# Layer 3's conditioning block: the second half of its routing one step sooner, and three row scatters per step

## The chip, the cores and the metric

The kernel runs on one core of one Trainium2 chip. The metric is device time in microseconds (us) for one execution of the whole program; shown is the median of several executions. The engines of a core each work through a queue of their own in order: TensorE (PE in the profile; its weight loads stand apart as PEld), VectorE (DVE), ScalarE (ACT), GpSimd (POOL) and SyncE (SP), which here only issues DMAs and reads registers. They meet through semaphores.

## The reference

Four layers follow one another on 2048 tokens of 256 channels. Each is `x = x + ffn(cond(x))`, and nearly all of these are mixtures of experts. The one that matters here is the condition of layer 3, cut to its core:

```python
shared = silu(xf @ w1) * (xf @ w3) @ w2              # all tokens, hidden width 512
s = sigmoid(concat([xf, tf], -1) @ router_W)         # 8 experts
_, topk_idx = top_k(s + router_bias, 2)
s_sel = take_along_axis(s, topk_idx, axis=1)
gates = s_sel / (s_sel.sum(axis=1, keepdims=True) + 1e-9)
h = gelu(einsum('nc,ech->enh', xf, W1e), approximate=False)
y = einsum('enh,ehc->enc', h, W2e)                   # hidden width 256
routed = einsum('ne,enc->nc', combine, y)            # combine: gates at the chosen two
out = (shared + routed) / 3
```

Every token goes through one shared expert and two routed ones of eight. The layers before it are complete when it starts, and the last expert layer, which sends each token to one of 16 experts, needs its result.

## The kernel before, in words

Tokens lie in SBUF twice: by channel (`XT`, for matmuls over channels) and by token (`Xt`, for rows). The 2048 tokens are 16 tiles of 128, and four blocks of 512.

A routed expert gets its tokens sorted. The kernel works out for each token and each of its two experts a row number in a DRAM buffer `xbuf`, scatters the token rows there (32 scatters: 16 tiles times two experts, each one indirect DMA that POOL issues), and then walks over 39 slots of 128 rows. A slot loads its rows (`xs`, line 297, issued by SP), turns them by a PE transpose (`ps_cm`, line 364), multiplies with its expert's weights (`cph`, line 1678, and `cpo`, line 1685) and scatters the result to another buffer, `tbuf`. The first `xs` load waits for all 32 scatters to have landed, since any of them may have written its rows.

To hide routing and scatters, they are spread over the shared expert. It takes blocks of 512 tokens; layer 3 runs three of the four blocks ahead of the slots (`lead` is 3) and the last one behind them. Its hidden width of 512 is four pieces of 128, so that a block is four steps, and three blocks are twelve. A step (`_shared`, lines 1413 to 1456) is: four matmuls for the gate (`spg`) and the up projection (`spu`), line 1440; a SiLU on ACT (`ssg`, line 1445); and the multiply on DVE (`sa`, line 1449). The down projection (`spo`, line 1426) of a step comes one step later, behind the next step's `spg` and `spu`, so that the multiply has time. Behind each `spo`, `_shared` calls a hook: the n-th hook comes in PE's queue behind the n-th `spo`, and so behind the `spg` and `spu` of step n + 1. The last step of a block is the exception (hooks 4, 8 and 12): its `spo` and hook follow at once, ahead of the next block.

The hooks drive a `Lead` (lines 303 to 333). The routing is a generator in two parts, split by `yield`. Part 1 computes the logits on PE (`ps_lt`), the sigmoid on ACT (`l3c_lt`), a transpose back (`l3c_pl`), and then on DVE the scores, the top two by MAX8 and FIND_INDEX8 (lines 173 and 175), one-hot masks `l3c_oh`, their sum `l3c_M` (line 1804) and its running sums over 16 tiles `l3c_cum` (line 193). Part 2 begins with matmuls on `l3c_M` and `l3c_cum` that count the rows before each token (`l3c_R` and `l3c_cnt`, lines 204 to 209), and goes on with some forty small DVE operations: the row numbers (`l3c_rows`), the expert of each slot (`l3c_eid`) and the gates. `Lead` gets the hooks at which the parts are issued, `at`, and a number of scatters per step, `per`:

```python
def hook(self, f, mul, mm):
    self.n += 1
    if self.n in self.at:
        self.part()
        if not self.at:
            for _ in range(min(self.per, len(self.sends))):
                self.sends.pop(0)()
    elif self.n > self.late:
        for _ in range(min(self.per, len(self.sends))):
            self.sends.pop(0)(mul)
```

At the hook of the last part the first `per` scatters are sent as soon as the row numbers are there; at each hook behind it `per` more, each of which also waits for that step's multiply `mul`. `late` is the largest number in `at`. With `(1, 3), 4`, part 1 is issued at hook 1, part 2 and four scatters at hook 3, and four at each of hooks 4 to 10.

What is left on the queues around this: SP reads the expert numbers of all slots into registers and loads the first slots' weights (`_slot_weights`, lines 1568 to 1577), then loads biases of the last layer over columns of `XT` that the shared blocks have finished with (line 2171, four loads of 128 KB for each block), and fetches `xs`. A planner turns the program into the engines' queues: it goes by the program's order where operands are ready by its own estimate of times, and lets later instructions pass where they are not. A queue's order is then fixed, and each engine keeps to it.

The other two layers that use `Lead` have eight pieces to a block and `(2, 4), 2`.

Of the kernel before, what the change touches and what calls it, by code (L numbers as in the profile page):

```python
# [78 lines left out]
def _bc(ap, axis, shape):  # L79
    return ap.unsqueeze(axis).to_broadcast(shape)  # L80
# [86 lines left out]
def _top(nc, pool, lg, E, name):  # L167

    m8 = pool.tile([P, NT, 8], F32, name=name + "_m8", tag="m8")
    ix = pool.tile([P, NT, 8], U32, name=name + "_ix", tag="ix")  # L170
    ixf = pool.tile([P, NT, 8], F32, name=name + "_ixf", tag="ixf")
    for t in range(NT):
        nc.vector.max(m8[:, t, :], lg[:, t, :])
    for t in range(NT):
        nc.vector.max_index(ix[:, t, :], m8[:, t, :], lg[:, t, :])
    nc.vector.tensor_copy(ixf, ix)
    return m8, ixf


def _one_hot(k, pool, ixf, n, E, name, tag=None):  # L180
    oh = pool.tile([P, NT, E], F32, name=name, tag=tag or name)
    k.nc.vector.tensor_tensor(oh, _bc(k.iota[:, 0:E], 1, [P, NT, E]),
                              ixf[:, :, n:n + 1].to_broadcast([P, NT, E]), ALU.is_equal)
    return oh


def _running(k, pool, M, E, name):

    nc = k.nc
    cum = pool.tile([P, NT + 1, E], F32, name=name + "_cum", tag="r_cum")  # L190
    nc.vector.memset(cum[:, 0, :], 0.0)
    for t in range(NT):
        nc.vector.tensor_add(cum[:, t + 1, :], cum[:, t, :], M[:, t, :])
    return cum
# [51 lines left out]
def _rows_of(k, pool, oh, pos, E, name, tag=None):  # L246

    nc = k.nc
    t = pool.tile([P, NT, E], F32, name=name + "_w", tag="rt")
    nc.vector.tensor_mul(t, oh, pos)  # L250
    f = pool.tile([P, NT], F32, name=name + "_f", tag="r_f")
    nc.vector.tensor_reduce(f, t, AX.X, ALU.add)
    u = pool.tile([P, NT], U32, name=name, tag=tag or name)
    nc.vector.tensor_copy(u, f)
    return u
# [1118 lines left out]
def _logits(k, psum, pool, src, w, E, name, dst, func=None, bias=None):  # L1374


    nc = k.nc
    ps = psum.tile([P, TB], F32, name="ps_lt", tag="mm")
    for c in range(2):
        for g in range(NB):  # L1380
            nc.tensor.matmul(ps[32 * g:32 * g + 32, :], w[:, c, :], src[:, c, g * TB:(g + 1) * TB],
                             start=c == 0, stop=c == 1, skip_group_check=True)
    lt = pool.tile([P, TB], F32, name=name + "_lt", tag="lt")
    if func is None:
        nc.scalar.copy(lt[:, 0:256], ps[:, 0:256])
        nc.vector.tensor_copy(lt[:, 256:TB], ps[:, 256:TB])
    else:
        nc.scalar.activation(lt, ps, func, bias=bias)
    pl = psum.tile([P, 4, 4, 32], F32, name=name + "_pl", tag="mm")
    for j in range(4):  # L1390
        nc.tensor.transpose(pl[:, j].rearrange("p g r -> p (g r)"), lt[:, j * P:(j + 1) * P], k.ident)
    nc.vector.tensor_copy(dst.rearrange("p (g j) e -> p j g e", g=4), pl[:, :, :, 0:E])
# [113 lines left out]
def _name_rows(k, rows, ixf, base):  # L1506

    k.nc.vector.tensor_scalar_add(rows[:, :, D], k.tok2, float(base))
    k.nc.vector.tensor_copy(rows[:, :, D + 1], ixf[:, :, 0])
# [162 lines left out]
def _gelu_products(k, pool, psum):  # L1672

    nc = k.nc

    def products(xT, R1, R2):
        ph = psum.tile([P, 2, P], F32, name="cph", tag="mm")
        made = [nc.tensor.matmul(ph[:, f, :], R1[:, c, f * P:(f + 1) * P], xT[:, c, :], start=c == 0,  # L1678
                                 stop=c == 1) for f in range(2) for c in range(2)]
        h = pool.tile([P, 2, P], F32, name="ch", tag="sg")  # L1680
        nc.scalar.activation(h, ph, AF.Gelu)
        yield made
        yield None
        po = psum.tile([P, D], F32, name="cpo", tag="o", bufs=2)
        made = [nc.tensor.matmul(po, h[:, f, :], R2[:, f, :], start=f == 0, stop=f == 1) for f in range(2)]  # L1685
        y = pool.tile([P, D], F32, name="ys", bufs=4)
        nc.vector.tensor_copy(y, po)
        yield made
        yield y
    return products  # L1690
# [93 lines left out]
def _cond_moe(k, name, wr, bias, W1, W3, W2, nf, hold, R1, R2, gate_mult, final, lead, next=None):  # L1784

    nc, A, XT, HT, Xt, Ht = k.nc, k.A, k.XT, k.HT, k.Xt, k.Ht
    rp, pool, psum = k.rp, k.pool, k.psum
    E, T, NS = 8, P, 39
    base = 0 if next else 8192
    w, rb = k.small[wr], k.small[bias]  # L1790
    sets = []
    for i in range(4):
        r = k.ring.take(1, hold).rearrange("p (n c f) -> p n c f", n=2, f=D)
        sets.append([(r[:, 0], A[R1]), (r[:, 1], A[R2])])
    def routing(lead_):
        s = rp.tile([P, NT, E], F32, name=name + "_s", tag="s")
        _logits(k, psum, rp, XT, w, E, name, s, AF.Sigmoid, k.small[wr, "b"])
        sel = rp.tile([P, NT, E], F32, name=name + "_sel", tag="lg")
        nc.vector.tensor_tensor(sel, s, _bc(rb, 1, [P, NT, E]), ALU.add)
        _, ixf = _top(nc, rp, sel, E, name)  # L1800
        _name_rows(k, k.Xr, ixf, base)
        oh = [_one_hot(k, rp, ixf, n, E, name + "_oh%d" % n, "oh%d" % n) for n in range(2)]
        M = rp.tile([P, NT, E], F32, name=name + "_M", tag="M")
        nc.vector.tensor_add(M, oh[0], oh[1])
        cum = _running(k, rp, M, E, name)
        yield
        pos, eid, of, _ = _route(k, rp, psum, M, cum, E, T, NS, len(sets), name)
        rows = [_rows_of(k, rp, oh[n], pos, E, name + "_rows%d" % n, "rows%d" % n) for n in range(2)]
        k.x.begin()
        lead_.sends = k.x.paced(k.Xr, rows)  # L1810

        nc.vector.tensor_mul(M, M, s)
        den = rp.tile([P, NT], F32, name=name + "_den", tag="den")
        nc.vector.tensor_reduce(den, M, AX.X, ALU.add)
        big = rp.tile([P, NT], F32, name=name + "_big", tag="big")
        nc.vector.tensor_single_scalar(big, den, 1e-9, ALU.is_gt)
        nc.vector.tensor_scalar_add(den, den, 1e-9)
        nc.vector.reciprocal(den, den)
        nc.vector.tensor_mul(den, den, big)
        nc.vector.tensor_scalar(big, big, -0.5, 0.5, ALU.mult, ALU.add)  # L1820
        gate = []
        for n in range(2):
            nc.vector.tensor_mul(oh[n], oh[n], s)
            g = rp.tile([P, NT], F32, name=name + "_g%d" % n, tag="g%d" % n)
            nc.vector.tensor_reduce(g, oh[n], AX.X, ALU.add)
            nc.vector.tensor_mul(g, g, den)
            nc.vector.tensor_add(g, g, big)
            nc.vector.tensor_scalar_mul(g, g, gate_mult * final)
            gate.append(g)
        lead_.made = gate, eid, of  # L1830

    def shared(tb, hook=None, mid=None, added=lambda: False):
        po = _shared(k, pool, psum, XT, tb, W1, W3, W2, nf, hook, mid)
        for i in range(2):
            t = tb * 4 + i * 2
            if added():
                nc.vector.scalar_tensor_tensor(Ht[:, t:t + 2, :], po[i], final, Ht[:, t:t + 2, :],
                                               ALU.mult, ALU.add)
            else:
                nc.scalar.activation(Ht[:, t:t + 2, :], po[i], AF.Copy, scale=final)  # L1840

    lead_ = Lead(k, routing, *((2, 4), 2) if nf == 8 else ((1, 3), 4))
    def hook(f, mul, mm):
        if k.late:
            k.late.pop(0)(k.silu, mul)
        lead_.hook(f, mul, mm)

    for tb in range(lead):
        shared(tb, hook)
    gate, eid, of = lead_.finish()  # L1850
    k.t.begin()
    slots = Series(k, Slots(k, pool, psum, of, base), 0, NS)
    for i in range(NS):
        slots.slot(i, _gelu_products(k, pool, psum), lambda: _slot_weights(k, eid, i, sets, E))
    slots.close()
    if next:
        next.begin()
    c = Tokens(k, pool, psum, gate, Ht, HT, nf, next)
    for tb in range(lead, NB):
        c.there = tb * 4  # L1860
        shared(tb, c.hook, c.hook, lambda: c.added >= tb * 4 + 4)
    c.there = NT
    k.ring.drop(hold)
    if next:
        next.finish(c)
    else:
        c.finish()
# [583 lines left out]
```

## Time and profile before

| | us |
|---|---|
| time, median of 3 runs | 1504.56 (1503.55 to 1510.06) |
| the profiled execution | 1522.55 |
| its span in the profile | 1520.8 |
| PE busy | 1448.3 (95%) |
| DVE busy | 468.9 (31%) |
| POOL busy | 280.9 (18%) |

The shares are of the span. Ends of matmuls are modelled, so a busy PE is not one at its peak. The mean clock that was granted to TensorE in the profiled execution was 0.977 of full speed. A line of the order in time reads: start in us from the span's start, duration in us, engine, source line, operation, tile written and tiles read, shapes and count; in brackets the time that the engine stood idle before it, and what ended that. "issue" there means that nothing the profile shows was waited for. "SPq" is a DMA issue on SP, so its duration is that of issuing and not of the transfer.

Layer 3's condition starts its shared blocks at 1176.0 us and its slots at 1258.4 us in that execution.

### The profile page before, as it was taken

Reading aid. Unit: us, or ns where it says so; the run is one execution under the profiler, and the core shown is the slowest. Engines: PE = TensorE matmul, PEld = TensorE weight load, DVE = VectorE, ACT = ScalarE, POOL = GpSimd, SP = SyncE. Lnnn points to the kernel's source line nnn. Section 1 sums busy time; section 2 is a strip of 40 time slices with the busy share of each in tenths; the row PEclk is TensorE's granted clock in tenths of the full one; section 3 lists DMA queues with packets and bytes.
Section 4 is the critical chain, followed back from the end, with each engine's and each line's share of the span. In section 5 each row is a group of like instructions: output and inputs, shape, how many; then the busy total and the mean of one; then the engine's idle time right before and its main releaser. Section 6 shows DMA issues by size and latency. Waiting matters only on the chain. (4 is left out here: it accounts for less than half of the span.)

```text
span 1520.8 us, 23724 instructions
## 1 busy us (share of the span) xinstructions
PE 1448.3 (95%) x8660; PEld 1023.3 (67%) x8660; DVE 468.9 (31%) x1606; ACT 304.9 (20%) x642; POOL 280.9 (18%) x317
## 2 busy tenths in 40 slices
PE   8999998999999999999999999999999969998897
PEld 4543333645557886555899999999976538864675
DVE  4432222325212444411211111111114404456432
ACT  3221111213111122211111111111112212135222
POOL 0400001200431440142010101010100253410442
PEclk9999999999999999999999999999999989998899
DMA  9669993943311772151235145246327438671470
GB/s 315 214 195 308 348 331 115 298 101 126 115 52 53 244 230 82 53 191 49 73 134 188 39 177 189 80 154 223 125 95 234 147 89 260 217 234 65 156 253 16
DMA packets 179856, 249.69 MB, mean 164 GB/s; under 512 B 17207, under 2 KB 132159, under 8 KB 179728
## 3 DMA queue, kind: packets, MB, share of 16 engines
q1 hardware_dynamic: 160064, 208.16, 42.5%
q0 software_dynamic: 14176, 36.63, 6.7%
q10 hardware_dynamic: 5488, 3.25, 0.7%
q8 instruction: 73, 1.20, 0.3%
q14 instruction: 55, 0.45, 0.1%
HBM read 284.86 MB, written 48.00 MB: 219 GB/s over the span
## 5 line engine op out<-in xcount | busy, mean ns | idle before, releaser
L281 POOL DMA_INDIRECT tbuf<-ys,sdst x114 | 112.2, 984 | 507.9 <-ACT ys L1714 382.6
L1426 PE MATMUL spo<-ring,sa 128*128 128x256 f32 x768 | 182.3, 382 | 12.9 <-DVE sa L1449 12.9
L1426 PEld LDWEIGHTS spo<-ring,sa 128*128 128x128 f32 x768 | 145.6, 191 | 63.0 <-issue 32.7
L1449 DVE TENSOR_TENSOR sa<-ssg,spu 128x512 f32<-128x512 f32 x96 | 65.8, 686 | 297.7 <-PE spu L1440 246.5
L1707 DVE TENSOR_TENSOR fa<-fsg,fpu 128x512 f32<-128x512 f32 x72 | 49.5, 688 | 316.2 <-PE fpu L1702 316.2
L1702 PE MATMUL fpg<-xsT,ring 128*128 128x128 f32 x1152 | 140.4, 275 | 0.7 <-issue 0.7
L1702 PE MATMUL fpu<-xsT,ring 128*128 128x128 f32 x1152 | 140.4, 275 | 0.0
L1702 PEld LDWEIGHTS fpg<-xsT,ring 128*128 128x128 f32 x1152 | 137.0, 192 | 2.7 <-issue 0.9
L1702 PEld LDWEIGHTS fpu<-xsT,ring 128*128 128x128 f32 x1152 | 134.4, 192 | 0.0
L1711 PE MATMUL fpo<-ring,fa 128*128 128x256 f32 x576 | 130.3, 379 | 0.0
L1445 ACT ACTIVATE ssg<-spg 128x512 f32<-128x512 f32 x96 | 57.3, 597 | 316.1 <-PE spg L1440 260.3
L1711 PEld LDWEIGHTS fpo<-ring,fa 128*128 128x128 f32 x576 | 106.7, 190 | 13.0
L1440 PE MATMUL spg<-HT,ring 128*128 128x512 f32 x192 | 95.9, 614 | 6.6 <-issue 3.5
L1440 PE MATMUL spu<-HT,ring 128*128 128x512 f32 x192 | 92.6, 605 | 0.0
L1440 PE MATMUL spg<-XT,ring 128*128 128x512 f32 x192 | 90.9, 595 | 0.1
L1440 PE MATMUL spu<-XT,ring 128*128 128x512 f32 x192 | 90.2, 592 | 0.0
L1678 PE MATMUL cph<-xsT,ring 128*128 128x128 f32 x624 | 84.2, 278 | 4.4 <-DMA ring<-in_L_r 2.7
L1678 PEld LDWEIGHTS cph<-xsT,ring 128*128 128x128 f32 x624 | 75.8, 191 | 8.6 <-issue 2.9
L1685 PE MATMUL cpo<-ring,ch 128*128 128x256 f32 x312 | 79.9, 380 | 0.0
L1706 ACT ACTIVATE fsg<-fpg 128x512 f32<-128x512 f32 x72 | 43.0, 597 | 171.7 <-PE fpg L1702 171.7
L1440 PEld LDWEIGHTS spu<-HT,ring 128*128 128x128 f32 x192 | 37.4, 196 | 46.7 <-issue 46.0
L1440 PEld LDWEIGHTS spu<-XT,ring 128*128 128x128 f32 x192 | 36.5, 190 | 45.9 <-issue 45.0
(580 smaller groups left out, 1637.4 us busy)
## 6 DMA issues: line engine op xcount, KB each, us to landing
ring<-in_L_w SPq DMA_DIRECT2D x108, 1024.0 KB
ring<-in_L_r SPq DMA_DIRECT2D x96, 512.0 KB
ring<-in_L_r SPq DMA_DIRECT2D x156, 256.0 KB
xs<-xbuf SPq DMA_DIRECT2D x138, 129.0 KB
ring<-in_L_W SPq DMA_DIRECT2D x32, 512.0 KB
yt<-tbuf SPq DMA_DIRECT2D x48, 256.0 KB
xbuf<-ACC SPq DMA_DIRECT2D x1, 3096.0 KB
ring<-in_L_s SPq DMA_DIRECT2D x6, 512.0 KB
```

What stands on the lines that cost most here:

```text
L281: i = k.nc.gpsimd.indirect_dma_start(out=self.ap, out_offset=bass.IndirectOffsetOnAxis(ap=idx, axis=0), in_=rows, in_offset=None, **end)
L1426: mm = nc.tensor.matmul(po[g // 2][:, g % 2, :], a[:, g * P:(g + 1) * P], W2[:, f, :], start=f == 0 and g % 2 == 0, stop=f == nf - 1, skip ...
L1440: mm = nc.tensor.matmul(ps, W[:, c, f * P:(f + 1) * P], X[:, c, cols], start=c == 0, stop=c == 1)
L1445: k.silu = nc.scalar.activation(sg, pg, AF.Silu)
L1449: mul = nc.vector.tensor_mul(a, sg, pu)
L1678: made = [nc.tensor.matmul(ph[:, f, :], R1[:, c, f * P:(f + 1) * P], xT[:, c, :], start=c == 0, stop=c == 1) for f in range(2) for c in ra ...
L1685: made = [nc.tensor.matmul(po, h[:, f, :], R2[:, f, :], start=f == 0, stop=f == 1) for f in range(2)]
L1702: made = [nc.tensor.matmul(ps[:, j, :], W[:, c, (f0 + j) * P:(f0 + j + 1) * P], xT[:, c, :], start=c == 0, stop=c == 1) for ps, W in ((pg, ...
L1706: nc.scalar.activation(sg, pg, AF.Silu)
L1707: nc.vector.tensor_mul(a[:, f0:f0 + 4, :], sg, pu)
L1711: made = [nc.tensor.matmul(po, a[:, f, :], W2[:, f, :], start=f == 0, stop=f == 4 * nh - 1) for f in range(4 * nh)]
```

## The change

One line of `_cond_moe` changes the arguments of `Lead` for layer 3's condition (the case `nf == 4`); layer 2's condition keeps its own.

```diff
-    lead_ = Lead(k, routing, *((2, 4), 2) if nf == 8 else ((1, 3), 4))
+    lead_ = Lead(k, routing, *((2, 4), 2) if nf == 8 else ((1, 2), 3))
```

Part 2 of the routing is issued at hook 2 in place of hook 3. Three scatters are sent there, three at each of hooks 3 to 11, and the two that remain at hook 12; before, it was four at each of hooks 3 to 10. No instruction is added or removed.

## The prediction

> **What bounds the kernel now.** I read the page first, then the order of instructions by time on each engine around layer 3's condition (about 1176 to 1262 us), then the waits. The page says that TensorE (PE) is the busy engine:
>
> ```profile
> span 1520.8 us, 23724 instructions
> PE 1448.3 (95%) x8660; PEld 1023.3 (67%) x8660; DVE 468.9 (31%) x1606; ACT 304.9 (20%) x642; POOL 280.9 (18%) x317
> ```
>
> So a change that touches no arithmetic can only move the places where PE stands. PE in this stage (start us, duration, engine, line, operation, tiles, count, idle before it and what ended that):
>
> ```profile
> 1191.83 1.89 PE L1426 MATMUL spo<-ring,sa 128*128 128x256 f32 x8
> 1193.56 1.88 PE L1440 MATMUL spg<-XT,ring 128*128 128x512 f32 x4
> 1195.28 1.88 PE L1440 MATMUL spu<-XT,ring 128*128 128x512 f32 x4
> ...
> 1198.72 0.39 PE L204 MATMUL l3c_R<-l3c_M,before 128*128 128x128 f32 x2
> ...
> 1232.74 3.78 PE L1426 MATMUL spo<-ring,sa 128*128 128x256 f32 x8 [12.55 <-DVE sa L1449]
> ...
> 1258.38 0.85 PE L364 MATMUL ps_cm<-ident,xs 128*128 128x128 f32 x4 [0.96 <-DMA xs<-xbuf]
> ```
>
> The reader should see three things. A step (spg, spu, spo) takes 5.16 us. The routing's second part begins with l3c_R, which follows the third step's spo. And the slots begin at 1258.38 with a wait for xs, rows that have come through DRAM: what ends last before the slots is the scatters, their landing and the load, though shared matmuls run until 1257.4 here.
>
> VectorE (DVE) shows what l3c_R needs:
>
> ```profile
> 1193.40 0.68 DVE L1449 TENSOR_TENSOR sa<-ssg,spu 128x512 f32<-128x512 f32 x1
> 1193.99 0.28 DVE L1804 TENSOR_TENSOR l3c_M<-l3c_oh,l3c_oh 128x128 f32<-128x128 f32 x1
> 1194.31 3.18 DVE L193 TENSOR_TENSOR l3c_cum<-l3c_cum,l3c_M 128x8 f32<-128x8 f32 x16
> 1197.41 0.68 DVE L1449 TENSOR_TENSOR sa<-ssg,spu 128x512 f32<-128x512 f32 x1
> ...
> 1254.07 0.69 DVE L1449 TENSOR_TENSOR sa<-ssg,spu 128x512 f32<-128x512 f32 x1 [4.47 <-PE spu L1440]
> ```
>
> The running sums are done at 1197.49, only 1.23 us before l3c_R starts. The scatters on GpSimd (POOL):
>
> ```profile
> 1203.11 1.04 POOL L281 DMA_INDIRECT xbuf<-Xt,l3c_rows  x1 [76.24 <-DVE l3c_ef L238]
> 1204.45 0.96 POOL L281 DMA_INDIRECT xbuf<-Xt,l3c_rows  x1 [0.30 <-issue]
> ...
> 1227.19 0.96 POOL L281 DMA_INDIRECT xbuf<-Xt,l3c_rows  x1 [0.30 <-issue]
> 1232.96 0.95 POOL L281 DMA_INDIRECT xbuf<-Xt,l3c_rows  x1 [4.82 <-DVE sa L1449]
> ...
> 1250.13 0.96 POOL L281 DMA_INDIRECT xbuf<-Xt,l3c_rows  x1 [0.30 <-issue]
> ```
>
> They run back to back, 1.263 us apart ((1227.19-1204.45)/18), so four fill 5.05 of a step's 5.16 us. The queue of DMA issues on SP:
>
> ```profile
> 1248.27 2.21 SPq L2171 DMA_DIRECT2D XT<-in_L_b  x4
> 1256.25 1.75 SPq L297 DMA_DIRECT2D xs<-xbuf  x4
> ```
>
> The last scatter left POOL at 1251.09; xs could be fetched only at 1256.25, 5.16 us later, with four bias loads in between on the same DMA engines.
>
> **A stall to take out first.** PE's 12.55 us wait hangs on ACT, whose wait the list of waits calls "remote", 19.1 us. In the trace's record of semaphore updates PE posts nothing from 1214.49 to 1231.35, then three updates within 0.1 us, although its matmuls were issued by 1218.30; SP's register loads slow at the same time from 0.56 to 2 to 3 us a triple. I take this for something that recording brings. The profiled execution took 1522.55 us against a median of 1504.56, 18 us more, and no other stall of that kind is in the trace. Without it everything on PE after 1232 comes 12.71 (1232.74 against 1218.30 + 1.73) + 1.85 (spo x8 took 3.58 to the next start, not 1.73) + 0.29 (spg x4) = 14.85 us earlier. POOL would not have waited (its releases stay ahead of it), so the 32nd scatter ends at 1204.45 + 30 x 1.263 + 0.96 = 1243.3, while shared matmuls end at 1257.42 - 14.85 = 1242.6. SP's remaining triples (35 x 0.56 us after 1213) would be over by about 1233 and the four bias loads behind them drained long before. So the scatters bound this stage in the runs that are timed. Their landing is then like layer 2's, where no bias load is near: last one out at 454.45, fetch at 456.20, 1.75 us. Slots begin at 1243.3 + 1.75 + 2.13 (1258.38-1256.25) = 1247.2, about 11 us before the profile's. The other 7 us of the 18 I leave to recording, unplaced; the sum is made as a difference in this stage and put on the median.
>
> **The change part by part.**
>
> *Part 2 at hook 2.* No instruction is added: 3 groups of matmuls and about 5.9 us of small DVE operations (1199.14 to 1205.0) move. In program order l3c_R would come behind the spo at 1191.83, at 1193.56. Its operand comes at 1197.49. If PE's queue holds it there, PE stands 3.93 us, and behind it stand spg and spu of the fourth step and their spo. If the planner sees that the sums are late, it puts spg and part of spu first; it does such things, since in layer 2 it put two l2f_pl at 623.36, two spg at 623.63 and two more l2f_pl at 624.50. A hint of its clock: it put the third step's sa (1193.40) just ahead of l3c_M, so it held that operand, whose spu ends 3.4 us after part 1's last transposes, ready by then; on the chip that point is 4.9 us after them. Its DVE is thus fast by some 1 to 2 us, and l3c_R lands early by about that. I take s = 1.0 us of PE standing, ends 0 and 3.93, nearer the planned placement. The scatters' start then moves by little: l3c_R to first scatter is 4.39 us (1203.11-1198.72), so from 1197.5 they begin at about 1202.0, 1.1 us sooner and not a step. The eid loads and the eight weight loads of SP start sooner by as much; the weights are not needed until the slots, over 40 us later, so that is hidden; if it weren't it would be a gain.
>
> *Three per step.* Before, 4 at hook 3 and 4 at each of hooks 4 to 10. After, 3 at hook 2, 3 at each of 3 to 11 (30), the last two at hook 12, waiting for the last multiply of the block. That wait is new. Those two are the last on POOL's queue; behind them stand only the fetches of xs. POOL by its own pace would be free at 1202.0 + 30 x 1.263 = 1239.9; the multiply ends at 1254.76 - 14.85 + s = 1240.9; an issue follows it after 0.27 us (as 1232.69 to 1232.96), so the two end at 1240.9 + 0.27 + 2.22 = 1243.4. Before: 1243.3. The 1.1 us of head start and the slack of the fewer scatters are eaten by the last release: +0.1, ends -0.9 (s = 0) and +3.0 (s = 3.93).
>
> *What is late next: the landing.* SP issues in order. The last four bias loads (before, at 1258.11, behind the first xs) wait only for the last spu, which ends ahead of the last multiply. Now that xs becomes ready only behind that multiply, I expect the planner to put the bias loads first. They then go out about 1240.2, 3.2 us ahead of the last scatter's end (before, in the profile, 2.8 ahead). The nearest row is therefore the profile's own 5.16 us, less 0.4 = 4.7 us; without them, 1.75. Here a rule of the Trainium skill stands against the row: "DMA: Bandwidth & Descriptors", Anatomy of one DMA, gives the software-issued DMA a nearly constant cost of about 2.0 us beyond its data. The layer-2 row agrees (1.75), the layer-3 row does not. By the rule landing is a constant and the change comes to +0.1 + 0.25, hardly anything; by the row it is +0.1 + (4.7 - 1.75) = +3.1. The same page's section on issuing engines says that DMAs of all queues interleave on the same 16 engines, which speaks against the change here. I take the row: 0 and +3.4 are its ends.
>
> **Sum:** 1504.56 + 3.1 = 1507.7 us, +0.2%. Slots, shared block 4 and the last layer follow in series and pass it on one for one. A measurement of this kernel can tell about 0.5%, 7.5 us, from no change: under 1497.0 is faster, over 1512.1 slower. A profiled execution should show 1525 or so if it stalls as this one did.
>
> **The rivals.**
>
> *PE is held in order (slower).* l3c_R sits at its program place: 3.93 us; and the fourth step's sa waits behind part 2's chain of 5.9 us (from 1198.4 to 1204.3, sa done 1205.0) so that its spo starts 1.7 us late: s = 5.6. Then 1243.4 + 4.6 + 4.7 against 1243.3 + 1.75 gives +7.7: 1512.2. It decides from s = 5.5 on; from there it is over 0.5%. For it: l3c_pl was placed ahead of its ACT and PE did wait 0.81 us at 1187.90. Against: the planner's reordering above.
>
> *The change doesn't bring part 2 forward.* The planner leaves l3c_R behind the third spo, where it now stands, because its cost for the sums is high. Scatters start at 1203.1 as before, the 32 end at 1243.3 as before, and only the landing may change: 0 to +3, 1506. For it: the slack of 1.23 us leaves little to gain.
>
> *The stall is real (faster).* If PE's silence belongs to twenty scatters back to back and not to recording, timed runs have it too, and gaps of 1.4 us in each step may end it. Before, slots at 1258.4; after, at 1243.4 + 4.7 + 2.1 = 1250.2: -8.2, 1496.4. For it: posting resumed 3.2 us after the stream paused at 1228.15. Against: the median is 18 us below the profiled time.
>
> **How the numbers follow.** The forecast 0.46 (its own range 1504 to 1511), PE held 0.26 (1508 to 1517, some 0.18 of it over 1512.1), unmoved 0.20, the stall 0.08 (0.07 under 1497). So faster 0.07, slower 0.18, the rest 0.75 within 0.5%. The range 1501 to 1514 leaves out the stall's case (0.08) and the upper end of PE held (0.10); it holds the bounds of s and of the landing.
>
> **What would show it.** In the changed profile: l3c_R after spg or within spu of the fourth step, between 1195 and 1198.5, with at most 2 us idle ahead of it; the first scatter near 1202; stretches of three scatters; the last two right behind the last sa; the bias loads ahead of the first xs on SP and over 4 us from the last scatter to xs. It is wrong if l3c_R waits 3 us or more, if xs follows the last scatter in 2 us, or if PE does not wait for xs at all, which would mean that the shared block and not the scatters bounds the stage.

## The result, and the profile after

| | before | after |
|---|---|---|
| time, median of 20 runs each | 1508.55 us (1502.80 to 1513.79) | 1513.18 us (1509.30 to 1519.44) |
| ratio to before, 95% interval | | 1.0034 [1.0023, 1.0044] |
| profiled execution | 1522.55 us | 1515.59 us |
| its span | 1520.8 us | 1513.9 us |

The change costs 0.34%, which is 5.1 us (3.5 to 6.6 by the interval). That lies within the 0.5% that the prediction called no change, though the interval of twenty runs each leaves out a ratio of 1. The two profiled executions stand the other way round, because the one of before held the stall that the prediction took out. So a second profile of the unchanged kernel is the partner in what follows; it is called "before again", has a span of 1506.0 us and no stall.

The page of the changed kernel shows the same work in the same shares (four matmul records are missing from this trace, 8656 against 8660 weight loads):

```profile
span 1513.9 us, 23722 instructions
PE 1447.7 (96%) x8656; PEld 1026.2 (68%) x8660; DVE 469.5 (31%) x1606; ACT 304.9 (20%) x642; POOL 280.8 (19%) x317
```

PE in the order of time, in layer 3's condition:

```profile
1183.84 1.89 PE L1426 MATMUL spo<-ring,sa 128*128 128x256 f32 x8
1186.44 0.46 PE L204 MATMUL l3c_R<-l3c_M,before 128*128 128x128 f32 x2 [0.71 <-DVE l3c_M L1804]
1189.36 0.49 PE L206 MATMUL l3c_R<-l3c_cum,ones 128*128 128x128 f32 x2 [2.46 <-DVE l3c_cum L193]
1189.68 0.36 PE L209 MATMUL l3c_cnt<-l3c_cum,ones 128*128 128x8 f32 x2
1189.89 3.63 PE L1440 MATMUL spg<-XT,ring 128*128 128x512 f32 x4
1193.36 1.88 PE L1440 MATMUL spu<-XT,ring 128*128 128x512 f32 x4
...
1236.36 3.62 PE L1426 MATMUL spo<-ring,sa 128*128 128x256 f32 x16
1244.88 1.37 PE L364 MATMUL ps_cm<-ident,xs 128*128 128x128 f32 x4 [4.91 <-DMA xs<-xbuf]
```

`l3c_R` stands right behind the second step's `spo`, where the program has it, and PE waits for its operands twice, 0.71 and 2.46 us. The `spg` behind it takes 3.47 us to the next start (1193.36 - 1189.89) where it takes 1.72 in the other steps. At the end PE waits 4.91 us for `xs`.

VectorE shows why the wait is as long as it is, and that the multiply of the fourth step isn't behind it:

```profile
1186.01 0.28 DVE L1804 TENSOR_TENSOR l3c_M<-l3c_oh,l3c_oh 128x128 f32<-128x128 f32 x1
1186.33 3.18 DVE L193 TENSOR_TENSOR l3c_cum<-l3c_cum,l3c_M 128x8 f32<-128x8 f32 x16
...
1195.35 0.69 DVE L1449 TENSOR_TENSOR sa<-ssg,spu 128x512 f32<-128x512 f32 x1 [0.61 <-PE spu L1440]
...
1236.63 0.69 DVE L1449 TENSOR_TENSOR sa<-ssg,spu 128x512 f32<-128x512 f32 x1 [4.47 <-PE spu L1440]
```

The running sums are finished at 1189.5, as PE gets going again. Before the fourth step's `sa` DVE is idle for 0.61 us and waits for `spu`, so that `sa` is late because PE is, and not because of DVE. POOL's scatters, the first and those around the end:

```profile
1193.70 1.04 POOL L281 DMA_INDIRECT xbuf<-Xt,l3c_rows  x1 [71.89 <-DVE l3c_ef L238]
...
1223.84 0.96 POOL L281 DMA_INDIRECT xbuf<-Xt,l3c_rows  x1 [3.40 <-DVE sa L1449]
...
1237.59 0.95 POOL L281 DMA_INDIRECT xbuf<-Xt,l3c_rows  x1 [1.67 <-DVE sa L1449]
1238.85 0.96 POOL L281 DMA_INDIRECT xbuf<-Xt,l3c_rows  x1 [0.30 <-DMA XT<-in_L_b]
```

POOL has gaps now, in which it waits for multiplies, 3.40 us in one; in before again none of its 31 gaps is longer than 0.31 us. The last two scatters go out 0.27 us behind the last multiply (1236.63 + 0.69 = 1237.32), and end at 1239.81. SP's DMA issues, with the bias loads now all ahead of the first `xs`:

```profile
1225.72 12.05 SPq L2171 DMA_DIRECT2D XT<-in_L_b  x9
1242.84 4.81 SPq L297 DMA_DIRECT2D xs<-xbuf  x6
```

To compare executions that begin this stage at different times, all times below are counted from the first `spg` of layer 3's condition (1169.49 us in before again, 1168.05 after):

| us after the first `spg` | before again | after | difference |
|---|---|---|---|
| first scatter | 27.07 | 25.65 | -1.42 |
| last multiply ends | 63.86 | 69.26 | +5.40 |
| last scatter ends | 67.35 | 71.75 | +4.40 |
| first `xs` is fetched | 69.53 | 74.78 | +5.25 |
| slots begin (`ps_cm`) | 71.59 | 76.83 | +5.24 |
| slots' length, first `ps_cm` to last `cph` | 82.81 | 83.37 | +0.56 |

The stage accounts for 5.24 + 0.56 = 5.8 us, against 5.1 (3.5 to 6.6) measured. The two spans themselves differ by 7.9 us, since in the one after the stage starts 1.44 us sooner and what follows the slots takes 3.5 us longer. Such differences come and go with no relation to the edit that shows: over ten profiles the stage's start moves between 1166.6 and 1176.0, and what follows the slots takes 181.8 to 185.7 us (185.2 in e6 below, which is the kernel before with some matmuls added, 183.0 in e4, which is the changed kernel with some added).

### The profile page after: what moved, and what is told of

It reads as the page before. It is cut to its first block, busy times and chain, and to the rows that moved or that the text cites. A ratio compares the mean times of both kernels' runs of the same rounds, so it can differ in the third digit from the quotient of the medians.

```text
span 1513.9 us, 23722 instructions
## 1 busy us (share of the span) xinstructions
PE 1447.7 (96%) x8656; PEld 1026.2 (68%) x8660; DVE 469.5 (31%) x1606; ACT 304.9 (20%) x642; POOL 280.8 (19%) x317
## 5 line engine op out<-in xcount | busy, mean ns | idle before, releaser
L1602 DVE COPY xsT<-ps_cm 128x256 f32<-128x256 f32 x138 | 57.1, 417 | 33.4 <-PE ps_cm L364 33.2
```

The source lines that it names most:

```text
L1602: turned = nc.vector.tensor_copy(xT, _channel_major(k, self.psum, xs, made=made))
```

## The experiments

All ratios are to the kernel before on the same chip. Each profile is one execution; e0 is one execution in all. To turn the lines shown into times from the stage's first `spg`: it stands at 1170.89 us in e1, 1168.61 in e2, 1174.02 in e3, 1170.31 in e4, 1166.57 in e5, 1171.90 in e6 and 1172.37 in e7. "Landing" is the time from the end of the last scatter on POOL to the first fetch of `xs`.

**e0, the kernel before once more.** No edit. It asks whether the stall belongs to the kernel.

> The kernel before, unchanged, for a second profile. In the first one PE's posts fell silent for 17 us at 1214 us, and the slots began 70.5 us after layer 3's l3c_pl (1258.38 against 1187.90). If that silence belongs to one recording, it is gone here: slots begin 59 to 60 us after l3c_pl, PE waits 4 to 5 us for xs ahead of them, the last scatter ends 55.4 us after l3c_pl and xs is fetched 1.8 us after it. If it belongs to the kernel, PE waits 12 us for the multiply again and the slots come at 70 us.

Measured: 1507.74 us, span 1506.0. PE's order in time at the slots, then the last multiply and the last scatter, then SP's:

```profile
1232.39 3.62 PE L1426 MATMUL spo<-ring,sa 128*128 128x256 f32 x16
1241.08 1.25 PE L364 MATMUL ps_cm<-ident,xs 128*128 128x128 f32 x4 [5.07 <-DMA xs<-xbuf]
```

```profile
1232.66 0.69 DVE L1449 TENSOR_TENSOR sa<-ssg,spu 128x512 f32<-128x512 f32 x1 [4.47 <-PE spu L1440]
1235.88 0.96 POOL L281 DMA_INDIRECT xbuf<-Xt,l3c_rows  x1 [0.30 <-issue]
```

```profile
1239.03 1.75 SPq L297 DMA_DIRECT2D xs<-xbuf  x4
1240.89 1.79 SPq L2171 DMA_DIRECT2D XT<-in_L_b  x4
```

There is no stall, and four `xs` loads go ahead of the last four bias loads. The slots begin 71.59 us after the first `spg`; the prediction had worked out 71.16 (1247.2 - 1176.04) for it. PE idles 5.07 us ahead of them: where there is no stall the scatters do bound the stage, as the prediction argued, and the shared matmuls don't.

**e1, the earlier half of the change alone: part 2 at hook 2, still four scatters per step.**

```diff
-    ... ((1, 3), 4))
+    ... ((1, 2), 4))
```

> Part 2 at hook 2 as in the changed kernel, but four scatters per step as before. PE is still held at l3c_R (3.2 us of waiting and a slow spg behind it, 5.4 us in all), but no scatter waits for the last multiply. Theory 'hold alone': the 5.4 us reach the end whatever the pace: ratio 1.003 or a little over. Theory 'both': the scatters end 54 us after l3c_pl, the shared block 60, so that PE no longer waits for xs; the hold eats the 4.6 us that PE used to wait: ratio 1.0006 (+0.9 us). Theory 'pace alone': nothing of the loss is left, ratio 0.999 to 1.000.

Measured: ratio 0.9987 [0.9978, 0.9997], about 2 us faster. PE at the slots, and the last scatter:

```profile
1239.19 3.62 PE L1426 MATMUL spo<-ring,sa 128*128 128x256 f32 x16
1242.65 0.60 PE L364 MATMUL ps_cm<-ident,xs 128*128 128x128 f32 x4
```

```profile
1235.79 0.96 POOL L281 DMA_INDIRECT xbuf<-Xt,l3c_rows  x1 [0.30 <-issue]
```

The hold at `l3c_R` is the same (last multiply at 69.26, exactly as after). But with four per step the scatters do not hang on the last multiplies: the last one ends at 65.85, 1.5 us sooner than before again, `xs` is fetched at 67.92, and PE doesn't wait for it. So the hold of 5.4 us comes out of PE's former wait of 5.07: the slots begin at 71.75 (+0.16), and last 79.94 us, not 82.81. The ratio alone would fit the theory "pace alone" (0.999 to 1.000); the profile decides for "both", as the hold is there and PE's wait takes it up. What "both" had left out is the 2.87 us that the slots gain. Moving part 2 alone is no loss; it becomes one only with three scatters per step.

**e2, the other half alone: three per step, part 2 where it was.**

```diff
-    ... ((1, 3), 4))
+    ... ((1, 3), 3))
```

> Part 2 at hook 3 as before, three scatters per step: hooks 3 to 12, and the last two right behind. No hold at l3c_R. Theory 'pace alone' and 'both': five scatters are left for the last multiply and behind, they end 58.3 us after l3c_pl and not 55.4, and the eight bias loads stand ahead of xs on SP, so that landing takes 3 us and not 1.75: +4.2 us, ratio 1.0028. Theory 'hold alone': ratio 1.000.

Measured: ratio 1.0005 [0.9992, 1.0018], less than expected. POOL's last scatters:

```profile
1232.74 0.96 POOL L281 DMA_INDIRECT xbuf<-Xt,l3c_rows  x1 [0.61 <-DVE sa L1449]
1234.00 0.96 POOL L281 DMA_INDIRECT xbuf<-Xt,l3c_rows  x1 [0.30 <-DMA XT<-in_L_b]
1235.27 0.96 POOL L281 DMA_INDIRECT xbuf<-Xt,l3c_rows  x1 [0.30 <-issue]
```

Only three scatters follow the last multiply, where the program's order has five: three at hook 12, and two left over for `finish`. The two wait for no multiply, and the planner put them ahead of the tied ones. The last ends at 63.86 + 0.27 + 2 x 1.263 + 0.96 = 67.62, 0.27 us later than before again. The landing took 3.06 us, not 2.18, as the bias loads went ahead of `xs`. Three per step alone costs next to nothing while the last multiply is on time. So by the times neither half of the change costs anything that can be told from nothing (e1 -2.0 us, e2 +0.8 with an interval across 0); the two together cost 5.1.

**e3, both parts one hook sooner: part 1 ahead of the block, part 2 at hook 2, four per step.** With 0 in `at`, `Lead` issues part 1 before the first shared step.

```diff
-    ... ((1, 3), 4))
+    ... ((0, 2), 4))
```

> Part 1 ahead of the first shared step, part 2 at hook 2, four scatters per step. The sums have two steps and a half until l3c_R, so PE is not held there; part 1 may wait about 1 us for the last columns of XT. l3c_R comes some 4.5 us sooner counted from the block's first spg, and the scatters with it: they end ahead of the shared block, and PE goes into the slots with 0 to 1 us of waiting instead of 4.6. If the scatters are what bounds the stage before the slots, -3 us, ratio 0.998; if the shared block already bounds it in timed runs, +1 us from the wait of part 1, ratio 1.0007.

Measured: ratio 0.9963 [0.9949, 0.9977], 5.6 us faster than before, so faster than both kernels. PE:

```profile
1186.05 1.89 PE L1426 MATMUL spo<-ring,sa 128*128 128x256 f32 x8
1187.78 0.38 PE L204 MATMUL l3c_R<-l3c_M,before 128*128 128x128 f32 x2
1188.00 0.39 PE L206 MATMUL l3c_R<-l3c_cum,ones 128*128 128x128 f32 x2
...
1188.37 1.96 PE L1440 MATMUL spg<-XT,ring 128*128 128x512 f32 x4
...
1233.16 3.62 PE L1426 MATMUL spo<-ring,sa 128*128 128x256 f32 x16
1236.62 0.88 PE L364 MATMUL ps_cm<-ident,xs 128*128 128x128 f32 x4
```

`l3c_R` stands at the same hook as after, but its operands are there: no wait, no slow `spg`. The scatters begin at 18.15 and end at 58.39, ahead of the last multiply at 60.10, so PE waits for no `xs` either. Counted from the stage's first matmul, which is now `ps_lt`, slots begin after 67.92 us in place of 71.59, and they last 80.46 in place of 82.81: 3.7 + 2.3 = 6.0 us. (Of the 5.07 us wait, some 1.5 are given back: the logits' 16 matmuls took 3.5 us here and 1.9 before; why is not shown.)

**e4, the changed kernel with the hold filled.** Fourteen bf16 matmuls that nobody reads are issued on PE ahead of `l3c_R`, so that PE stands still for less.

```diff
         yield
+        if nf == 4:
+            _warm(k, psum, k.hook_mm, 14, tag="t", bufs=2)
         pos, eid, of, _ = _route(k, rp, psum, M, cum, E, T, NS, len(sets), name)
...
+        k.hook_mm = mm
         lead_.hook(f, mul, mm)
```

> The changed kernel, with 14 matmuls on constants (their result is read by nobody) in PE's queue just ahead of l3c_R, where PE stands for about 3.8 us. The wait for the sums stays as long as it was, but PE is not idle in it. If the slow spg behind the wait (3.47 us instead of 1.72) is the price of having stood still, it is back at 1.72, the last multiply and the last scatters come 1.75 us sooner and the slots too: ratio to before 1.0022 instead of 1.0034. If it is not, nothing changes.

Measured: ratio 1.0015 [1.0005, 1.0024]. PE:

```profile
1187.82 3.19 PE L1406 MATMUL warm<-ident 128*128 128x512 bf16 x14
1190.84 0.38 PE L204 MATMUL l3c_R<-l3c_M,before 128*128 128x128 f32 x2
1191.60 0.49 PE L206 MATMUL l3c_R<-l3c_cum,ones 128*128 128x128 f32 x2 [0.38 <-DVE l3c_cum L193]
...
1192.11 1.96 PE L1440 MATMUL spg<-XT,ring 128*128 128x512 f32 x4
1193.91 1.88 PE L1440 MATMUL spu<-XT,ring 128*128 128x512 f32 x4
```

The sums are no earlier, and the second pair of `l3c_R` starts as late (21.30 us after the first `spg`; 21.31 without the filling). But the `spg` behind it takes 1.80 us, not 3.47, the last multiply comes 1.70 us sooner (67.56) and the slots 1.46 (75.37). The clock granted to PE between 1192 and 1194 is 1.00. So a third of what the hold cost was TensorE's clock and not the waiting.

**e5, the changed kernel with four bias loads behind the first `xs` loads.** Two of each eight bias loads, which had gone ahead of `xs`, wait for the fourth `xs` load, which gives SP the order that before again has. (The lines that keep the `xs` loads by number are left out.)

```diff
...
-            nc.sync.dma_start(self.b2[:, e, :], k.A["L3_b2"][e:e + 1].to_broadcast([P, D]))
+            i = nc.sync.dma_start(self.b2[:, e, :], k.A["L3_b2"][e:e + 1].to_broadcast([P, D]))
+            if e % 8 in (4, 5):
+                _behind(k, i, k.xs_load[3])
```

> The changed kernel, with the four bias loads of the third block's columns placed behind the first four xs loads on SP, as they are in the kernel before. Theory 'bias loads delay the landing': xs is fetched 2.2 us after the last scatter's end instead of 3.0, and the slots begin 0.8 us sooner. Theory 'the landing is what it is': 3.0 us again. The time itself can hardly tell 0.8 us; the profile can.

Measured: ratio 1.0023 [1.0012, 1.0034]. The last scatter, and SP:

```profile
1237.36 0.96 POOL L281 DMA_INDIRECT xbuf<-Xt,l3c_rows  x1 [0.30 <-issue]
```

```profile
1240.38 1.75 SPq L297 DMA_DIRECT2D xs<-xbuf  x4
1242.24 1.79 SPq L2173 DMA_DIRECT2D XT<-in_L_b  x4
```

The last scatter ends at 71.75 as after, and `xs` is fetched 2.07 us behind it in place of 3.03. The bias loads' share of the landing is therefore 0.96 us in this pair of profiles, and the slots begin 0.82 sooner. The two ratios' intervals overlap, so the time alone doesn't show it; the profile does.

**e6, the kernel before with PE kept busy ahead of the slots.** Sixteen unread bf16 matmuls are issued between the last `spo` and the slots.

```diff
+        k.hook_mm = mm
         lead_.hook(f, mul, mm)
...
     gate, eid, of = lead_.finish()
+    if nf == 4:
+        _warm(k, psum, k.hook_mm, 16, tag="t", bufs=2)
```

> The kernel before, with 16 matmuls on constants (their result is read by nobody) between the shared blocks and the first slot, where PE waits 3.7 to 5 us for xs. Scatters, landing and xs come as before, so the slots begin at the same point, 71.6 us after the block's first spg. If standing still costs PE its clock, the first slots now run at full clock and the slots take 80 us and not 83: -2.9 us, ratio 0.998. If not, 1.000.

Measured: ratio 0.9991 [0.9977, 1.0005]. PE:

```profile
1238.26 3.62 PE L1406 MATMUL warm<-ident 128*128 128x512 bf16 x16
1243.70 0.89 PE L364 MATMUL ps_cm<-ident,xs 128*128 128x128 f32 x4 [1.82 <-DMA xs<-xbuf]
```

The slots begin when they did (71.79 against 71.59) but last 80.57 us in place of 82.81. By the profile the wait's after-effect on the clock is 2.2 us; the timed runs can't separate their 1.4 from nothing.

**e7, the changed kernel with part 2 between step 4's matmuls and step 3's `spo`.** It is the place that the prediction thought the planner would choose: behind `spg` and `spu` of the fourth step.

```diff
+        if nf == 4 and lead_.n == 1:
+            return
         lead_.hook(f, mul, mm)
...
+    def mid(f, mul, mm):
+        if nf == 4 and lead_.n == 1 and f == 3:
+            lead_.hook(f, mul, mm)
...
-        shared(tb, hook)
+        shared(tb, hook, mid)
```

> The changed kernel with part 2 placed behind the spu of the fourth step, where the forecast had assumed it, instead of behind the second spo; still three scatters per step. PE is held half a us at most. Then the last multiply ends 64.4 us after the block's first spg (changed kernel 69.3), the last scatter 66.9 (71.8), and with a landing of 3.0 us xs is fetched at 69.9 and the slots begin at 72.0 (76.8; before 71.6). Ratio 1.000. If the pace and not the hold were the loss, the slots would stay at 76 to 77 and the ratio at 1.003.

Measured: ratio 1.0010 [1.0001, 1.0018], slots at 72.29. PE:

```profile
1191.60 1.88 PE L1440 MATMUL spu<-XT,ring 128*128 128x512 f32 x4
1193.32 0.38 PE L204 MATMUL l3c_R<-l3c_M,before 128*128 128x128 f32 x2
1193.67 0.49 PE L206 MATMUL l3c_R<-l3c_cum,ones 128*128 128x128 f32 x2
```

No wait at all, the first scatter at 25.78 (25.65 after) and the last multiply at 64.09, within 0.23 us of before again. With only the hold taken away, the slots come 4.54 us sooner than after. What remains over before again, 0.70 us, is mostly the landing: 3.47 us in place of 2.18, on scatters that end 0.76 sooner.

Set side by side, the stage explains the times (differences to before again, us):

| | slots begin | slots' length | sum | measured, 95% interval |
|---|---|---|---|---|
| after | +5.24 | +0.56 | +5.8 | +5.1 (3.5 to 6.6) |
| e1 | +0.16 | -2.87 | -2.7 | -2.0 (-3.3 to -0.5) |
| e2 | +1.19 | +1.17 | +2.4 | +0.8 (-1.2 to 2.7) |
| e3 | -3.67 | -2.35 | -6.0 | -5.6 (-7.7 to -3.5) |
| e4 | +3.78 | +0.02 | +3.8 | +2.3 (0.8 to 3.6) |
| e5 | +4.42 | -1.36 | +3.1 | +3.5 (1.8 to 5.1) |
| e6 | +0.20 | -2.24 | -2.0 | -1.4 (-3.5 to 0.8) |
| e7 | +0.70 | -0.53 | +0.2 | +1.5 (0.2 to 2.7) |

Seven of the eight sums lie in the interval beside them; e4's lies 0.2 us above it. The measured column is (ratio - 1) times the median of before beside it (1508.55 us for after, 1507.9 for e1 to e3, 1510.24 for e4 to e7).

## Why the prediction was right or wrong

The total was near: +3.1 us forecast, +5.1 measured, and the absolute 1513.18 lies in the range of 1501 to 1514. Of the 5.5 us between 1507.7 and 1513.18, 4.0 are the median of before, which is 1508.55 over 20 runs and was 1504.56 over three; so of the stalled profile's excess, 14.0 us over that median, about 3 remain unplaced and not 7. But that the sum came out so near is in part luck: of its two terms the scatters' end was too small by 4.3 us (+0.1 forecast, +4.40 measured) and the landing too large by 2.1 (+2.95 against +0.85), and the two errors partly cancelled.

**What bounds the kernel: right.** The stall was peculiar to that one execution. Nine other profiles have none of it in this stage, none of the 127 timed runs of the kernel before took longer than 1516.30 us against its 1522.55, and the unstalled stage was worked out to 0.4 us. Calling it an effect of recording goes further than the runs do: the others were recorded as well. Why it happened stays open; the rival "the stall is real" is refuted.

**Part 2 at hook 2, the value of s: wrong; this step failed.** The text put s at 1.0 us, with 3.93 as its upper end, on the hint that the planner would see the sums come late. It did not: `l3c_R` stands at its program place. (What the planner's own clock gave for the sums is not on record, so why it left them there stays open.) The wait of 3 us or more that was named as the sign of an error is there in two pieces, 0.71 + 2.46 = 3.17 us. Measured at the last multiply, s was 5.40 us, beyond its own upper end. The parts: from the second `spo` to `spg` 6.05 us in place of 1.73, less the 0.59 that the group used to take at its old place, is 3.73, near the 3.93 of the bound. The `spg` behind it took 3.47 in place of 1.72: 1.75 more. The two make 5.48. The clock that was granted to PE is in the table of stretches (stretch, its length; busy time and instructions of PE, PEld, DVE, ACT, POOL; granted clock; DMA share; GB/s), here of after:

```profile
1184.00:1190.00 6.00, 2.83 (x16) 2.12 (x14) 5.18 (x32) 0.00 (x0) 0.00 (x0) 0.99 0.00 0
1190.00:1194.00 4.00, 4.00 (x7) 1.77 (x7) 3.92 (x27) 0.44 (x1) 0.30 (x1) 0.59 0.01 2
```

The clock falls as the hold ends, so the work behind a wait pays for it. If the clock is always either full or half, the two rows come to about 3.4 us at half clock (an estimate: 2 x 0.01 x 6.00 + 2 x 0.41 x 4.00). This bound left the clock out; e4, which fills the wait, gets 1.70 of the 1.75 back. The Trainium skill has the rule in "TensorE: Matmul & The Clock Gate", Part 1: The HAM clock gate: after an idle window of about 3.4 us the clock drops to half until the engine has been busy for about as long. The trace agrees on the drop and on the 3.4 us until the clock is back; the idle time that it shows before the drop is less than the page's, 3.17 us and broken by two matmuls. The rule was not weighed in the prediction, and should have been: the four matmuls of `spg`, 1.72 us together, would take twice that at half clock, which makes the upper end of s 3.93 + 1.72 = 5.65 (an estimate with that page's rule), just over the 5.5 us from which the slower rival decided. e7, in which `l3c_R` is put where the prediction assumed it, shows the rest: s falls to 0.23 and the slots come at 72.29.

**The first scatter: right.** 1.1 us sooner was forecast, 1.42 measured; a hook of 5.16 us sooner in the program is not a step sooner on the chip.

**The last two scatters tied to the last multiply: mechanism right, size off through s.** With the measured s the text's own formula gives 63.86 + 5.40 + 0.27 + 2.22 = 71.75, and 71.75 was measured. It forecast +0.1 for the scatters' end; it was +4.40. That this tie is what passes the hold on is shown by e1, which has the hold and four per step and loses nothing, and by e2, which has the tie and no hold.

**Landing: direction right, size wrong.** The planner did put the bias loads ahead of `xs`. But they cost 0.96 us (e5), not 2.95: the landing went from 2.18 to 3.03 us. The row of 5.16 us came from the stalled execution; no other profile comes near it, and what drew it out is not shown. The rule of the Trainium skill that was weighed against it, about 2.0 us constant from "DMA: Bandwidth & Descriptors", Anatomy of one DMA, was much the better for the landings without bias loads ahead (2.07 to 2.27 in before again, e1, e3, e5 and e6), and too low by 1 to 1.5 us for those with them (3.03 to 3.47 in after, e2, e4 and e7). Neither was the value to take; about 3 was.

**The rivals.** "PE is held in order" had the place of `l3c_R` and, at 5.6 us, the size of s, but not for its reason. It added 1.7 us for a fourth `sa` kept back by part 2's chain on DVE; in the profile after, that `sa` waits for `spu`, and the 1.75 us are the clock. Its total was too high (+7.7 against +5.1), because it carried the long landing. "The change doesn't bring part 2 forward" is refuted by the same lines of PE.

**What would show it.** Seen: the first scatter near its place (25.65 us after the first `spg`, 25.96 forecast), the last two scatters right behind the last `sa`, the bias loads ahead of `xs`, PE waiting for `xs`. Not seen: `l3c_R` behind `spg`; at least 4 us of landing; stretches of three scatters from the start (the first 18 run back to back, as they begin too late to meet a multiply that isn't done).

## What to carry to other kernels

A consumer moved to an earlier place in an in-order queue helps only as far as its operand is earlier: compare the operand's ready time with the new place first, and then move the producer too, as e3 does. Price an engine's standing still with what comes behind it, the clock included, and don't count on a planner to step around it. A transfer tied to the last step of a stage hands on every delay of that stage, where an untied one had slack; and a landing time should not be taken from an execution that shows a stall.

## What the runs showed of the hardware

PE's wait for `xs` costs more than its length. The clock granted ahead of the slots and at their start, in before again:

```profile
1236.00:1241.00 5.00, 0.01 (x1) 0.00 (x0) 0.00 (x0) 1.88 (x2) 0.84 (x1) 0.88 0.34 102
1241.00:1244.00 3.00, 2.92 (x12) 2.27 (x13) 1.21 (x6) 0.00 (x0) 0.00 (x0) 0.50 0.88 194
1244.00:1247.00 3.00, 3.00 (x15) 2.94 (x15) 0.65 (x3) 0.77 (x2) 0.00 (x0) 0.57 0.76 185
1247.00:1250.00 3.00, 3.00 (x24) 2.75 (x23) 1.55 (x6) 0.38 (x1) 0.99 (x1) 1.00 0.79 244
```

and in e6, which differs by the matmuls that fill most of the wait:

```profile
1243.70:1246.70 3.00, 2.85 (x22) 2.43 (x23) 1.75 (x9) 0.38 (x1) 0.00 (x0) 1.00 0.61 184
```

PE works at half clock for about 5.6 us, against full clock in e6. With the 1.2 us before it has work again, that makes 6.8 us at half clock (an estimate, worked out as above from the first three rows). The same working, over all ten profiles, gives only three sizes: no half clock ahead of and in the slots for waits up to 1.82 us, about 3.5 us behind e5's wait of 4.09 us (as behind the hold), and 6.7 to 6.9 us behind the waits of 4.9 us and over. These are one and two times the window of about 3.4 us that the same page's rule gives, so in these profiles the price of a wait comes in steps. Over all ten profiles the length of the slots goes roughly with the wait ahead of them:

| PE's wait for `xs`, us | slots' length, us |
|---|---|
| none (e1, e3), 0.96 (the first profile of before), 1.82 (e6) | 79.94, 80.46, 80.58, 80.57 |
| 4.09 (e5) | 81.45 |
| 4.91 (after), 5.07 (before again), 5.15 (e4), 5.54 (e7), 6.26 (e2) | 83.37, 82.81, 82.83, 82.28, 83.98 |

Up to 1.8 us of wait costs the slots nothing that shows here, 5 to 6 us cost them some 2 to 3.5 us. Only e6 changes the wait's filling and nothing else, so it alone shows the cause; the rest agree with it. It is part of why e1 and e3, which end the wait, gain more than the wait's own length would let one expect.
